# Attention kernel on one core: the values matmuls of quadrants 1 and 3 joined, and one VectorE addition put later

## Chip, core and metric

The kernel runs on one core of a Trainium2 chip. The metric is the device time of one execution in microseconds (us); lower is better. The kernel before takes 1030.06 us (median of three runs, 1028.61 to 1030.34).

## What is computed

The input is 64 sequences of 128 tokens with 512 features. The layer normalises the tokens, projects them to 16 query heads of 64 and to one shared key and value of 64, adds a null key and value, a bias per head, a causal mask and a padding mask, takes the softmax, weighs the values, projects back to 512, normalises again and adds the input:

```
xn = layernorm(x, g_in)
q = (xn @ Wq).reshape(b, n, H, DH).transpose(0, 2, 1, 3) * scale
kv = xn @ Wkv                        # k, v, with the null row ahead of each
sim = jnp.einsum('bhid,bjd->bhij', q, k) + bias      # causal and padding masks
attn = jax.nn.softmax(sim, axis=-1)
out = jnp.einsum('bhij,bjd->bhid', attn, v)
out = out.transpose(0, 2, 1, 3).reshape(b, n, INNER) @ Wo
return x + layernorm(out, g_out)
```

## The kernel before

All is float32. The 64 sequences are worked in pairs: step d (0 to 31) takes sequences a = 2d and b = 2d + 1 through scores and softmax, and the pair before, p = 2d - 2 and p + 1, through values and output projection. Each engine works its instructions in the order in which the code records them; nothing is reordered by a planner. A step is a call of `turn(d)` and then of `body_full(d)` (d = 4 to 29; earlier steps use `body`, the last two `turn_end` and `body_end`).

`turn` gives TensorE a thick run of small matmuls: `scores` (L765 to L786) for both sequences on quarters of the array, 64 rows by 64 columns, then `values` (L891 to L919) on eighths, 32 rows by 64 columns. In `values`, quadrant s of four holds 32 query tokens' weights; `turns` says in which order its blocks of keys are taken, each entry being (block j, first place, number of places). An entry with two places is one matmul of 256 columns for each half r, an entry with one place is one of 128. For s = 1 and 3, block j = 1 is two matmuls of 128; `wide` names the quadrants for which the two are made one of 256. `WIDE` (L889) names quadrant 3 alone, and `turn` (L1109, L1110) hands it to p in steps 5 to 29, and to p + 1 in the odd ones of these and in 14 and 24. So a sequence has 32 values matmuls (four rounds, four quadrants, two halves), less two for each quadrant joined.

`body_full` gives TensorE some 25 us of large matmuls: key and value projection (`kv_pair`), the query projection of the next group in a seven-product scheme (`product_two`), whose products 2, 3 and 4 are worked in the same way once more (`inner_products`), and the output projection (`out_product`), also of seven products. VectorE reads the products out of PSUM and adds them up: `inner_out` (L725) into the query tile `qT`, `q_out_two` (L621), and `out_part` (L1032) into the output `y`. Every float32 matmul that the code writes stands in the program as two weight loads and two matmuls, and both engines of the trace, PEld for loads and PE for matmuls, are fed by TensorE's one instruction stream. Some of its waits are instructions of their own: 11 in an even full step, 5 in an odd one. An even step has 780 loads and matmuls in all (772 in 14 and 24, 788 in step 4), an odd one 772.

At the end of the step, `inner_products(4, g, h, (4, 3))` (L1647) writes again into areas A0 and A1 of the fourth product's PSUM tile, which VectorE must have read by then (`inner_out(4, ...)`, L1643 and L1644). Ahead of these two readings VectorE has `q_out_two(g, h, 0, 1, "c", "u2")` (L1639), which reads another PSUM tile, `pc`.

Of the kernel before, what the change touches and what calls it, by code (L numbers as in the profile page):

```python
# [17 lines left out]
def kernel(  # L18
# [460 lines left out]
    def q_next(g, h):  # L479
        q_tiles(g, h, [q_tags[g - 1, j, h] for j in range(2)])  # L480
# [6 lines left out]
    def q_whole(g, j, u, h):  # L487
        return qT[g, j, h][:, :, :, :, u, :]
# [130 lines left out]
    def q_out_two(g, j, u, h, tag, name):  # L619
        v, k = KEPT[name]  # L620
        nc.vector.tensor_tensor(  # L621
            q_whole(g, j, u, h).rearrange("p f t h i -> p (f t h) i"),
            prod[tag].rearrange("p f (n i) -> p (f n) i", i=DH),
            q_whole(g, j, v // HC, k).rearrange("p f t h i -> p (f t h) i"),
            ALU.add,
        )
# [163 lines left out]
    def scores_add(b, hf):  # L790
        sv = S[b][:, :, KEYS[hf]].rearrange("p (r f) j -> p r f j", r=2)
        pv = pss.pop((b, hf))
        if isinstance(pv, list):
            for r in (1, 0):
                nc.vector.tensor_tensor(sv[:, r], pv[r], sv[:, r], ALU.add)  # L795
        else:
            nc.vector.tensor_tensor(sv, pv, sv, ALU.add)
# [88 lines left out]
            ps_y.tile(shape, FP, tag="X", name=f"po_{p + 1}_3"),  # L886
        ]

    WIDE = (3,)  # L889

    def values(b, wide=()):  # L891

        g, t = divmod(b, GB)
        sb = sbs.pop(b)
        po = pos[b]
        turns = (
            ((0, 0, 2), (1, 1, 1), (2, 1, 1), (3, 1, 1)),
            ((0, 0, 2), (1, 0, 1), (1, 1, 1), (2, 1, 1)),
        )
        for turn in range(len(turns[0])):  # L900
            for s in range(NQ):
                j, to, n = turns[s % 2][turn]
                if s in wide and j == 1:
                    if turn == 2:
                        continue
                    n = 2
                quad = slice(s * Q, (s + 1) * Q)
                slots = slice(2 * to + j, 2 * to + j + 2 * n - 1, 2)
                for r in range(2):
                    rows = slice(r * DH, (r + 1) * DH)  # L910
                    nc.tensor.matmul(  # L911
                        po[s][rows, to : to + n],
                        vr[g][quad, t, PLACE[j], :],
                        sb[quad, slots, r * NF : (r + 1) * NF, :],
                        start=(turn == 0),
                        stop=True,
                        skip_group_check=(turn > 0),
                        tile_position=(s * Q, r * DH),
                    )  # L919
# [144 lines left out]
    def pair_gain(b):  # L1064
        nc.vector.tensor_tensor(yn[b], yn[b], gob, ALU.mult)
# [23 lines left out]
    PAIRS = B // 2  # L1089
    late_T = []  # L1090

    def turn(d):

        a, b, p = 2 * d, 2 * d + 1, 2 * d - 2
        g = d // 2 + 1
        homes = (ps_y, "Y"), (ps_q, "a")
        if d == 1:
            homes = homes[::-1]
        scores(a, 0, (homes[0], (ps_w, "w")))
        scores(b, 0, (homes[1], (ps_w, "w")))  # L1100
        scores(a, 1)
        scores(b, 1, ((ps_y, "X"), (ps_q, "c")))
        scores_add(a, 0)
        scores_add(b, 0)
        scores_max(a, 0)
        scores_add(a, 1)
        scores_add(b, 1)
        po = values_rooms(p)
        values(p, WIDE if 4 < d < PAIRS - 1 else ())  # L1109
        values(p + 1, WIDE if 4 < d < PAIRS - 1 and (d % 2 or d % 10 == 4) else ())  # L1110
        if d % 2 and (d + 1) // 2 < NG:
            mask_neg((d + 1) // 2)
        bias_add(a + 2)
        if d % 2 == 0:
            token_sum(g, 1)
            token_sum(g, 2)
        exps(a, 0)
        values_out(p, po)
# [403 lines left out]
    def body_full(d):  # L1522

        a, b, p, l = 2 * d, 2 * d + 1, 2 * d - 2, 2 * d - 4
        g, h = d // 2 + 1, d % 2
        xw = g + 1 < NG
        m = (g + 1) * GB + 2 * h
        sums = h == 0
        q_next(g, h)
        pkv = kv_pair(g * GB + 2 * h)  # L1530
        scores_max(b, 0)
        rinv(a, 0)
        scale(a, 0)
        on = two_stats((ys[l], ys[l + 1]), "o")
        if sums:
            token_sums_inner(g, 2)
            token_sum(g, 3)
        kv_pair_out(g * GB + 2 * h, pkv)
        if h == 1 and xw:
            load_mask(g + 1)  # L1540
        nmrs[l], nmrs[l + 1] = two_nmr(*on, "o")
        if xw:
            xn = two_stats((xs[m], xs[m + 1]), "x")
        scores_max(a, 1)
        product_two(g, h, 1, ps_q, "a")
        keep_two("a", g, h, "p1")
        pair_norm(l)
        inner_room(2, g, h)
        inner_products(2, g, h, (1,))
        inner_out(2, g, h, "00")  # L1550
        exps(b, 0, 0, 1)
        scores_max(b, 1)
        if xw:
            xnmr[m], xnmr[m + 1] = two_nmr(*xn, "x")
        pair_gain(l)
        pair_residual(l)
        store(l)
        out_sum(p, 0)
        if sums:
            token_sum(g, 4)  # L1560
        out_product(p, 1, ps_y, "X")
        out_keep(p, "X", "yp1")
        out_sum(p, 1)
        out_sum(p, 2)
        exps(b, 0, 1, 4)
        product_two(g, h, 6, ps_q, "a", start=False)
        pair_norm(l + 1, (ps_y, "Y"))
        keep_two("a", g, h, "u2")
        if xw:
            norm_apply(m)  # L1570
        product_two(g, h, 5, ps_q, "c")
        exps(b, 0, 4)
        pair_gain(l + 1)
        inner_products(2, g, h, (6,))
        inner_out(2, g, h, "01")
        out_product(p, 2, ps_w, "w")
        out_part(p, 0, "w")
        out_sum(p, 3)
        if xw:
            norm_apply(m + 1)  # L1580
            tokens_T(m)
        pair_residual(l + 1)
        store(l + 1)
        rinv(b, 0)
        if xw:
            tokens_T(m + 1)
            if h == 1:
                tokens_out(g + 1)
                tokens_in(g + 1)
        for r in (p, p + 1):  # L1590
            load_res(r)
        if m + 2 < B and xw:
            load_x(m + 2)
            load_x(m + 3)
        exps(a, 1, 0, 4)
        product_two(g, h, 7, ps_q, "a", start=False)
        keep_two("a", g, h, "u3")
        inner_products(2, g, h, (7, 5, 2))
        inner_out(2, g, h, "11")
        inner_out(2, g, h, "00,11")  # L1600
        if sums:
            token_sums_inner(g, 3)
            token_sums_inner(g, 4)
        inner_room(3, g, h)
        inner_products(3, g, h, (1,))
        q_out_two(g, h, 1, 1, "c", "u3")
        inner_out(3, g, h, "00")
        out_product(p, 5, ps_y, "Y")
        exps(a, 1, 4)
        rinv(a, 1)  # L1610
        scale(a, 1)
        scale(b, 0)
        out_keep(p, "Y", "yp5")
        inner_products(3, g, h, (6, 5))
        inner_out(3, g, h, "01")
        inner_products(2, g, h, (4, 3))
        inner_out(2, g, h, "01,10")
        inner_room(4, g, h)
        inner_products(4, g, h, (1,))
        inner_out(4, g, h, "00")  # L1620
        exps(b, 1, 0, 3)
        if h == 1:
            values_T(g)
        out_product(p, 6, ps_y, "X", start=False)
        out_keep(p, "X", "yu2")
        inner_products(3, g, h, (7,))
        exps(b, 1, 3)
        blocks_T(a)
        rinv(b, 1)
        scale(b, 1)  # L1630
        bias_add(b + 2)
        if d == PAIRS - 3:
            bias_add(B - 1)
        inner_products(4, g, h, (6,))
        inner_out(4, g, h, "01")
        inner_out(3, g, h, "1*")
        inner_out(3, g, h, "*1")
        inner_products(3, g, h, (2, 3, 4))
        q_out_two(g, h, 0, 1, "c", "u2")  # L1639
        out_product(p, 7, ps_y, "X", start=False)  # L1640
        out_part(p + 1, 1, "X")
        inner_products(4, g, h, (7, 5, 2))
        inner_out(4, g, h, "11")  # L1643
        inner_out(4, g, h, "00,11")  # L1644
        out_product(p, 3, ps_y, "Y", start=False)
        out_part(p, 1, "Y")
        inner_products(4, g, h, (4, 3))  # L1647
        inner_out(4, g, h, "01,10")
        if d == PAIRS - 3:
            pair_stats(p)  # L1650
            pair_pow(p)
        blocks_T(b)
        out_product(p, 4, ps_y, "X", start=False)
        out_part(p + 1, 0, "X", False)
# [179 lines left out]
```

## Time and profile before

| | us |
|---|---|
| median of three runs | 1030.06 |
| the profiled execution | 1030.99 |
| its span from first to last instruction | 1029.2 |
| PE busy | 1019.0 |
| PEld busy | 899.0 |
| DVE busy | 860.5 |
| POOL busy | 775.3 |
| ACT busy | 674.4 |

PE is TensorE's matmuls, PEld its weight loads, DVE VectorE, ACT ScalarE, POOL GpSimd. An instruction's name gives its line in the kernel and, with an arrow, the tile that it writes and those that it reads. Idle time of an engine stands with what ended it; "issue" means that the profile shows nothing that the engine waited for. The windows view gives the length of a stretch, then each engine's busy time with the number of its instructions in brackets. Steps are cut here at the first weight load of their scores.

### The profile page before, as it was taken

How to read it: one execution, taken by the hardware profiler on the slowest of the kernel's cores; microseconds unless marked ns; L12 is line 12 of the kernel's file. 1: busy time of each engine (PE TensorE's matmuls, PEld its weight loads, DVE VectorE, ACT ScalarE, POOL GpSimd, SP SyncE). 2: the span in 40 equal slices, each digit the busy share in tenths (PEclk: the TensorE clock that was granted, in tenths of full speed). 3: DMA queues.
4: the chain of work that ended last, by engine and by line, in shares of the span. 5: the costliest groups of instructions: out<-in, count | busy, mean ns of one | idle time of the engine just before them, and what ended most of it. 6: DMA issues, size and time to landing. Idle time of an engine off the chain costs nothing.

```text
span 1029.2 us, 31577 instructions
## 1 busy us (share of the span) xinstructions
PE 1019.0 (99%) x12489; PEld 899.0 (87%) x12489; DVE 860.5 (84%) x1849; ACT 674.4 (66%) x2675; POOL 775.3 (75%) x621
## 2 busy tenths in 40 slices
PE   9999999999999999999999999999999999999997
PEld 8888888888888888888888888888988888888886
DVE  6877778888888888889888898888888888878788
ACT  5766677656577566686656776566765657856583
POOL 4997779687686876959768596786968769687686
PEclk9999999999999999999999999999999999999999
DMA  7415143151521415225152341514314152141221
GB/s 218 137 30 152 64 132 99 45 144 64 147 93 68 122 57 151 86 69 130 49 160 76 100 122 37 160 66 135 99 54 134 63 151 89 69 101 35 69 83 62
DMA packets 73835, 100.87 MB, mean 98 GB/s; under 512 B 32212, under 2 KB 36056, under 8 KB 71896
## 3 DMA queue, kind: packets, MB, share of 16 engines
q1 hardware_dynamic: 73392, 98.47, 32.1%
q8 instruction: 98, 1.61, 0.7%
q14 instruction: 49, 0.40, 0.1%
q10 hardware_dynamic: 296, 0.40, 0.1%
HBM read 63.19 MB, written 33.55 MB: 94 GB/s over the span
## 4 chain that ended last, share of the span: by engine, by line
PE 96%; POOL 1%; ACT 1%; DVE 1%; issue 1%; DMA 0%; POOLq 0%; DVEq 0%
PE pyX L998 19%; PE pa L603 13%; PE pi L697 11%; PE pyY L998 10%; PE po L911 8%; PE pkv L404 6%; PE pyw L998 5%; PE pc L603 4%; PE ps L780 3%; PE pq L499 3%; PE pa L554 2%; PE sc_X L780 2%; PE sc_Y L780 2%; PE pc L697 2%; PE pc L554 1%; PE sc_a L780 1%
## 5 line engine op out<-in xcount | busy, mean ns | idle before, releaser
L811 ACT ACTIVATE s<-s,nmax 128x65 f32<-128x65 f32 (+1 forms) x1024 | 370.9, 366 | 62.1 <-DVE nmax L802 62.1
L833 POOL TENSOR_TENSOR s<-s,rinv 128x512 f32<-128x512 f32 (+1 forms) x132 | 189.7, 1448 | 117.8 <-DVE rinv L829 117.8
L745 POOL TENSOR_TENSOR s<-biasp,mneg 128x1552 f32<-128x1552 f32 (+1 forms) x65 | 206.3, 3176 | 34.0 <-DVE s L795 22.5
L811 ACT ACTIVATION_READ_ACCUMULATOR s<-s,nmax 128x1 f32 x1024 | 194.5, 190 | 0.0
L725 DVE TENSOR_TENSOR qT<-pi,qT 128x128 f32<-128x128 f32 (+1 forms) x376 | 123.4, 340 | 39.4 <-PE pi L697 31.1
L1034 ACT COPY y<-pyX 128x256 f32<-128x256 f32 x29 | 10.8, 373 | 184.3 <-PE pyX L998 184.3
L802 DVE TENSOR_REDUCE nmax<-s 128x8 f32<-128x1032 f32 (+1 forms) x128 | 121.7, 951 | 0.1
L849 DVE STREAM_TRANSPOSE sb<-s 128x1536 f32<-128x1536 f32 (+1 forms) x68 | 113.7, 1675 | 2.1 <-POOL s L833 1.7
L998 PE MATMUL pyX<-wo,oT 128*128 128x256 f32 x464 | 109.7, 379 | 0.0
L998 PE MATMUL pyX<-wT,oT 128*128 128x256 f32 x464 | 109.7, 379 | 0.0
L978 POOL TENSOR_TENSOR oT<-oT 128x512 f32<-128x512 f32 x64 | 81.3, 1278 | 27.8 <-PE pyw L998 25.5
L998 PEld LDWEIGHTS pyX<-wo,oT 128*128 128x128 f32 x464 | 84.0, 190 | 9.2
L998 PEld LDWEIGHTS pyX<-wT,oT 128*128 128x128 f32 x464 | 84.0, 190 | 9.2
L911 PE MATMUL po<-sb,vr 32*64 32x128 f32 (+1 forms) x3904 | 88.8, 309 | 2.7 <-issue 2.4
L911 PEld LDWEIGHTS po<-sb,vr 32*64 32x64 f32 x3904 | 73.9, 131 | 15.5 <-issue 11.0
L930 ACT ACTIVATE oT<-po,nv 128x512 f32<-128x512 f32 (+1 forms) x127 | 74.1, 661 | 3.4 <-PE po L911 3.2
L404 PE MATMUL pkv<-xT,wkv 128*128 128x256 f32 x256 | 63.3, 391 | 0.0
L998 PE MATMUL pyY<-wo,oT 128*128 128x256 f32 x256 | 60.5, 379 | 0.0
L998 PE MATMUL pyY<-wT,yS 128*128 128x256 f32 x256 | 60.5, 379 | 0.0
L998 PE MATMUL pyw<-wo,oT 128*128 128x256 f32 x256 | 60.5, 379 | 0.0
L614 ACT COPY qT<-pa 128x512 f32<-128x512 f32 x78 | 45.4, 583 | 18.5 <-PE pa L603 18.3
L404 PEld LDWEIGHTS pkv<-xT,wkv 128*128 128x128 f32 x256 | 46.2, 189 | 10.0 <-DVE s L795 2.1
(231 smaller groups left out, 2509.0 us busy)
## 6 DMA issues: line engine op xcount, KB each, us to landing
res<-in_x_dram SPq DMA_DIRECT2D x64, 256.0 KB
out_dram<-y SPq DMA_DIRECT2D x63, 256.0 KB
x<-in_x_dram SPq DMA_DIRECT2D x62, 256.0 KB
xd<-xb SPq DMA_DIRECT2D x14, 1024.0 KB
xT<-xd SPq DMA_DIRECT2D x56, 256.0 KB
vr<-vd SPq DMA_DIRECT2D x64, 128.0 KB
kT<-kT SPq DMA_DIRECT2D x32, 64.0 KB
vd<-vb SPq DMA_DIRECT2D x32, 64.0 KB
```

Of the source, the lines that this page charges most:

```text
L404: nc.tensor.matmul(pkv, wkv[:, kc, :], xT[g][:, t : t + 2, kc, :], start=(kc == 0), stop=(kc == KC - 1),)
L603: nc.tensor.matmul(prod[tag][:, i], w[:, kc, f * P : (f + 1) * P], t[:, :, kc, :], start=first, stop=(kc == HK - 1), skip_group_check=not ...
L697: nc.tensor.matmul(to, inner_w[k][i][:, h], inner_x[k, g][i], start=(i == 1), stop=True, skip_group_check=(i != 1),)
L725: nc.vector.tensor_tensor(o, p, o, ALU.add)
L745: nc.gpsimd.tensor_tensor(S[b][:, :, keys], biasp[:, :, keys], mneg[:, t, keys] .unsqueeze(1) .broadcast_to([P, R8, keys.stop - keys.start ...
L780: nc.tensor.matmul(home[r][u * DH : (u + 1) * DH, f, :], qT[g, f // 2, t // 2][rows, f % 2, t % 2, hf, u], kT[rows, 0 : nk // Q, t, :], st ...
L802: nc.vector.tensor_reduce(nmax[b][:, hf], S[b][:, :, WITH_NULL[hf]], AX.X, ALU.max, negate=True)
L811: nc.scalar.activation(row, row, AF.Exp, bias=nmax[b][:, hf, k : k + 1], accum_out=rsum[b][:, hf, k : k + 1],)
L833: nc.gpsimd.tensor_tensor(sv, sv, rinvs[b, hf][:, lo:hi].unsqueeze(2).broadcast_to([P, hi - lo, sv.shape[2]]), ALU.mult,)
L849: nc.vector.transpose(sbs[b][:, :, lo:hi].rearrange("p j e q -> p e j q"), S[b][:, lo:hi, 1 : ROW - 1].rearrange("p e (j k) -> p e j k", k=Q),
L911: nc.tensor.matmul(po[s][rows, to : to + n], vr[g][quad, t, PLACE[j], :], sb[quad, slots, r * NF : (r + 1) * NF, :], start=(turn == 0), st ...
L998: nc.tensor.matmul(prod[key], h[:, c, :], w[:, c, :], start=(start and c == 0), stop=(c == HC - 1), skip_group_check=not start,)
```

## The change

```diff
-    WIDE = (3,)
+    WIDE = (1, 3)
...
-        values(p, WIDE if 4 < d < PAIRS - 1 else ())
-        values(p + 1, WIDE if 4 < d < PAIRS - 1 and (d % 2 or d % 10 == 4) else ())
+        steady = 3 < d < PAIRS - 2
+        values(p, WIDE if steady else ())
+        values(p + 1, (WIDE if d % 2 else WIDE[1:]) if steady else ())
...
-        q_out_two(g, h, 0, 1, "c", "u2")
         out_product(p, 7, ps_y, "X", start=False)
         out_part(p + 1, 1, "X")
         inner_products(4, g, h, (7, 5, 2))
         inner_out(4, g, h, "11")
         inner_out(4, g, h, "00,11")
+        q_out_two(g, h, 0, 1, "c", "u2")
         out_product(p, 3, ps_y, "Y", start=False)
```

In steps 4 to 29, p now has quadrants 1 and 3 joined, p + 1 both in an odd step and quadrant 3 in an even one. An odd step goes from 772 to 756 loads and matmuls, an even one to 764. With the waits that stand by themselves, whose number does not change, that is 761 and 775 instructions, 1536 for two steps, 768 for one on average; before it was 777 and 791 (783 in 14 and 24), 1568 for two.

TensorE, in the values of an odd step, sequence p, from the second round of `turns` on (po_0 to po_3 are the four quadrants' PSUM tiles; each row stands for the halves r = 0 and 1). Before:

```order
L911 MATMUL po_0_7945<-sb_7825,vr_7411 64x128 x2
L911 MATMUL po_1_7946<-sb_7825,vr_7411 64x128 x2
L911 MATMUL po_2_7947<-sb_7825,vr_7411 64x128 x2
L911 MATMUL po_3_7948<-sb_7825,vr_7411 64x2x128 x2
L911 MATMUL po_0_7945<-sb_7825,vr_7411 64x128 x2
L911 MATMUL po_1_7946<-sb_7825,vr_7411 64x128 x2
L911 MATMUL po_2_7947<-sb_7825,vr_7411 64x128 x2
L911 MATMUL po_0_7945<-sb_7825,vr_7411 64x128 x2
L911 MATMUL po_1_7946<-sb_7825,vr_7411 64x128 x2
L911 MATMUL po_2_7947<-sb_7825,vr_7411 64x128 x2
L911 MATMUL po_3_7948<-sb_7825,vr_7411 64x128 x2
```

TensorE at the same place, with the change:

```order
L911 MATMUL po_0_7885<-sb_7765,vr_7355 64x128 x2
L911 MATMUL po_1_7886<-sb_7765,vr_7355 64x2x128 x2
L911 MATMUL po_2_7887<-sb_7765,vr_7355 64x128 x2
L911 MATMUL po_3_7888<-sb_7765,vr_7355 64x2x128 x2
L911 MATMUL po_0_7885<-sb_7765,vr_7355 64x128 x2
L911 MATMUL po_2_7887<-sb_7765,vr_7355 64x128 x2
L911 MATMUL po_0_7885<-sb_7765,vr_7355 64x128 x2
L911 MATMUL po_1_7886<-sb_7765,vr_7355 64x128 x2
L911 MATMUL po_2_7887<-sb_7765,vr_7355 64x128 x2
L911 MATMUL po_3_7888<-sb_7765,vr_7355 64x128 x2
```

Quadrant 1's second matmul has 256 columns and its third row is gone; the columns that each quadrant streams are the same.

VectorE at the end of an even step (L725 is `inner_out`, L621 `q_out_two`, L1032 `out_part`, L849 the next transposition; pi_10_1_8192 is the fourth product's tile). Before:

```order
L725 TENSOR_TENSOR qT_1_1_8028<-pi_10_1_8167,qT_1_1_8028 128x2x2x64
L621 TENSOR_TENSOR qT_1_1_8028<-pc_1_5_8112,qT_1_1_8028 128x8x64
L1032 TENSOR_TENSOR y_8184<-pyX_1_8092,y_8184 128x256
L725 TENSOR_TENSOR qT_1_0_8027<-pi_10_1_8192,qT_1_0_8027 128x2x64
L725 TENSOR_TENSOR qT_1_0_8027<-pi_10_1_8192,qT_1_0_8027 128x2x2x64
L1032 TENSOR_TENSOR y_8097<-pyY_5_8171,y_8097 128x256
L725 TENSOR_TENSOR qT_1_0_8027<-pi_10_1_8192,qT_1_0_8027 128x4x64
L849 STREAM_TRANSPOSE sb_8252<-s_7830 128x8x6x32
```

VectorE at the same place, with the change:

```order
L725 TENSOR_TENSOR qT_1_1_7964<-pi_10_1_8103,qT_1_1_7964 128x2x2x64
L1032 TENSOR_TENSOR y_8120<-pyX_1_8028,y_8120 128x256
L725 TENSOR_TENSOR qT_1_0_7963<-pi_10_1_8128,qT_1_0_7963 128x2x64
L725 TENSOR_TENSOR qT_1_0_7963<-pi_10_1_8128,qT_1_0_7963 128x2x2x64
L621 TENSOR_TENSOR qT_1_1_7964<-pc_1_5_8048,qT_1_1_7964 128x8x64
L1032 TENSOR_TENSOR y_8033<-pyY_5_8107,y_8033 128x256
L725 TENSOR_TENSOR qT_1_0_7963<-pi_10_1_8128,qT_1_0_7963 128x4x64
L849 STREAM_TRANSPOSE sb_8188<-s_7770 128x8x6x32
```

The addition that reads `pc` stands three places later, behind the two readings of the fourth product's tile. No other engine's order changes, and no DMA moves.

## The prediction

> **What bounds the kernel now.** I read the page first: the engines' busy time, the clock, the chain that ended last and the queues.
>
> ```profile
> PE 1019.0 (99%) x12489; PEld 899.0 (87%) x12489; DVE 860.5 (84%) x1849; ACT 674.4 (66%) x2675; POOL 775.3 (75%) x621
> PEclk9999999999999999999999999999999999999999
> PE 96%; POOL 1%; ACT 1%; DVE 1%; issue 1%; DMA 0%; POOLq 0%; DVEq 0%
> q8 instruction: 98, 1.61, 0.7%
> ```
>
> TensorE is busy for 99% of the span at full clock and is 96% of the chain. So only its own work, or its own idle time, can change the time by much. The last row matters here: queue q8 brought 98 packets of instructions, 1.61 MB, so 16.4 KB each. TensorE's program has 2 x 12489 loads and matmuls and 261 others, 25239 in all; over 98 packets that is 257 to a packet. I take it as one block of 256 instructions at a time.
>
> Next the waits, all lines on the places that the change touches:
>
> ```profile
> PEld po L911 <- issue: 11.0, 44, 0.8
> PEld pi L697 <- DVE qT L725: 3.9, 13, 0.3
> PE po L911 <- issue: 2.4, 7, 0.5
> ```
>
> At the values (po, L911) TensorE stood idle 13.4 us and waited for nothing that the profile shows, up to 0.8 us at a time. At the fourth product (pi, L697) it waited for VectorE. To see how much of the first is loss, I cut the span at steps with the windows view (length, then busy time and count by engine):
>
> ```profile
> 185.85:970.45 784.60, 782.10 (x9691) 691.20 (x9690) 667.00 (x1449) 519.53 (x2047) 584.21 (x467) 1.00 0.32 96
> 154.83:185.85 31.02, 31.02 (x396) 27.56 (x395) 26.75 (x58) 20.28 (x81) 28.34 (x26) 1.00 0.28 87
> 342.64:374.62 31.98, 31.46 (x392) 27.75 (x391) 26.54 (x59) 20.41 (x81) 28.51 (x27) 1.00 0.28 89
> 595.25:626.46 31.21, 31.21 (x392) 27.71 (x391) 27.11 (x59) 20.38 (x81) 28.52 (x27) 1.00 0.28 90
> 626.46:658.05 31.59, 31.50 (x387) 27.66 (x386) 26.96 (x60) 21.43 (x83) 18.70 (x12) 1.00 0.38 105
> 658.05:689.10 31.05, 31.05 (x392) 27.59 (x391) 27.18 (x59) 20.29 (x81) 28.51 (x26) 1.00 0.29 93
> 689.10:720.18 31.08, 31.08 (x387) 27.54 (x386) 26.86 (x60) 21.31 (x83) 18.71 (x12) 1.00 0.39 111
> 782.31:814.14 31.83, 31.44 (x387) 27.74 (x387) 26.71 (x59) 20.29 (x81) 28.56 (x26) 1.00 0.27 86
> ```
>
> The first row is steps 5 to 29 together; then come steps 4, 10, 18, 19, 20, 21 and 24. Undisturbed, an even step takes 31.05 us (step 20) and an odd one 31.08 (step 21), yet equal work takes up to 31.98 (step 10). The 25 steps in the first row would take 13 x 31.08 + 12 x 31.05 = 776.6 us undisturbed; they took 784.60. So **8.0 us** is lost in them. The timeline of weight loads shows where:
>
> ```profile
> 285.41 0.22 PEld L911 LDWEIGHTS po<-sb,vr 32*64 32x64 f32 x11 [0.67 <-issue]
> 348.28 0.44 PEld L911 LDWEIGHTS po<-sb,vr 32*64 32x64 f32 x27 [0.77 <-issue]
> 788.05 0.19 PEld L911 LDWEIGHTS po<-sb,vr 32*64 32x64 f32 x3 [0.63 <-issue]
> 850.34 0.41 PEld L911 LDWEIGHTS po<-sb,vr 32*64 32x64 f32 x19 [0.22 <-issue]
> ```
>
> In the middle of the values, between two loads of one kind, the stream stops for 0.2 to 0.8 us, each time at another place (11, 27, 3, 19 loads are left). I counted what lies from gap to gap:
>
> ```profile
> 285.40:348.27 62.87, 62.35 (x760) 55.11 (x760) 53.55 (x119) 41.61 (x164) 47.20 (x39) 1.00 0.33 99
> 788.04:850.33 62.29, 62.28 (x760) 55.07 (x760) 52.95 (x117) 40.97 (x162) 46.67 (x38) 1.00 0.33 100
> ```
>
> Both times 760 loads: with as many matmuls and the 16 waits that two steps hold, 1536 instructions, six blocks of 256. The gaps stand at the seams of the blocks that q8 brings: the stream has run dry. Before the change two steps hold 1568, so a seam falls 32 earlier in each later pair of steps, and drifts through the thick run of scores and values.
>
> **The seams after the change.** Two steps hold 1536, so every even step has its seams where step 4 has them, which nothing ahead of it moves. Loads from the start of steps 4, 18, 19, 20 and 21 to a gap:
>
> ```profile
> 154.82:285.40 130.58, 129.94 (x1798) 115.20 (x1797) 113.17 (x244) 86.51 (x346) 99.38 (x79) 1.00 0.34 99
> 595.24:788.04 192.80, 192.33 (x2574) 170.50 (x2573) 167.61 (x362) 128.28 (x510) 146.75 (x118) 1.00 0.33 100
> 626.45:788.04 161.59, 161.12 (x2184) 142.80 (x2183) 140.50 (x304) 107.90 (x429) 118.23 (x91) 1.00 0.34 102
> 658.04:788.04 130.00, 129.63 (x1798) 115.13 (x1797) 113.54 (x245) 86.47 (x346) 99.53 (x80) 1.00 0.34 101
> 689.09:788.04 98.95, 98.58 (x1408) 87.55 (x1407) 86.36 (x187) 66.19 (x265) 71.02 (x53) 1.00 0.35 103
> ```
>
> Step 4: 2 x 1797 and 34 waits are 3628 = 14 x 256 + 44, so its seams stand at instructions 44, 300 and 556, early in the scores, early in the values and in the body. Step 20 has the same count, so the same seams; both took the undisturbed time (31.02 and 31.05). The odd steps follow 775 instructions later, 7 over three blocks, so their seams stand at 37, 293 and 549. By the same count (23, 39 and 50 waits) step 21 has 21 and 277 and lost nothing; step 19 has 53 and 309 and lost 31.59 - 31.08 = 0.51 us; step 18, an even one, has 76 and 332 and lost 0.16. An odd step's 37 lies midway between 21 and 53: I take 0.2 us left for each of 13 odd steps and none for the even ones, 2.6 us. The bounds are 0 (all like steps 20 and 21) and 0.51 x 13 + 0.16 x 13 = 8.7 us.
>
> The Trainium skill, page "Runtime: NRT & Kernel Launch", section "Instruction fetch mechanics", gives the same block, 16 KiB or 256 instructions. It also says that crossing such a boundary is "mostly hidden"; the gaps of 0.63 to 0.77 us at the seams speak against that here. What it would give is the first rival.
>
> **The joined matmuls.** 102 matmuls of the code are saved, 408 instructions, 25239 to 24831. The columns stay. Does the values block itself get shorter? Undisturbed blocks with none, two and four joined, each row pair from its first load to that of the next kind:
>
> ```profile
> 157.67 2.28 PEld L911 LDWEIGHTS po<-sb,vr 32*64 32x64 f32 x128 [0.17 <-issue]
> 160.12 0.94 PEld L404 LDWEIGHTS pkv<-xT,wkv 128*128 128x128 f32 x5 [0.17 <-DVE s L795]
> 660.89 2.31 PEld L911 LDWEIGHTS po<-sb,vr 32*64 32x64 f32 x124 [0.17 <-issue]
> 663.37 0.94 PEld L404 LDWEIGHTS pkv<-xT,wkv 128*128 128x128 f32 x5 [0.17 <-DVE s L795]
> 691.94 2.29 PEld L911 LDWEIGHTS po<-sb,vr 32*64 32x64 f32 x120 [0.17 <-issue]
> 694.40 0.94 PEld L404 LDWEIGHTS pkv<-xT,wkv 128*128 128x128 f32 x5 [0.17 <-DVE s L795]
> ```
>
> 128 loads take 2.45 us, 124 take 2.48, 120 take 2.46: the columns set the time, not the number of instructions. I count the joining by itself at **0**. It is covered by the other quadrants' streaming; the ends are 26 x 0.03 = +0.8 us (as from 128 to 124) and, if instructions set it after all, 204 loads x 2.31/124 = -3.8 us. The rows name 0.17 us ahead of the values in each step; that stays, and is no part of the 8.0.
>
> **The areas read sooner.** The end of an even (748) and an odd step (779), TensorE and then VectorE:
>
> ```profile
> 747.13 1.89 PE L998 MATMUL pyY<-wo,oT 128*128 128x256 f32 x8
> 749.40 0.38 PE L998 MATMUL pyX<-wT,oT 128*128 128x256 f32 x1
> 778.15 1.89 PE L998 MATMUL pyY<-wo,oT 128*128 128x256 f32 x8
> 780.49 0.38 PE L998 MATMUL pyX<-wT,oT 128*128 128x256 f32 x1
> ```
>
> ```profile
> 748.00 0.74 DVE L725 TENSOR_TENSOR qT<-pi,qT 128x128 f32<-128x128 f32 x2
> 778.21 0.69 DVE L621 TENSOR_TENSOR qT<-pc,qT 128x512 f32<-128x512 f32 x1
> 779.14 0.74 DVE L725 TENSOR_TENSOR qT<-pi,qT 128x128 f32<-128x128 f32 x2
> 780.08 0.42 DVE L1032 TENSOR_TENSOR y<-pyY,y 128x256 f32<-128x256 f32 x1 [0.19 <-PE pyY L998]
> ```
>
> Eight matmuls at 0.216 us (the eight from 747.13 end by 749.02, 0.38 of it the last one's own length: 1.51 / 7) and four half as wide at 0.111 us (an estimate: half of the first and 3 ns) are 2.17 us; from the first pyY to pyX it was 2.27 and 2.34. TensorE loses 0.10 us in an even step and 0.17 in an odd one, since the four matmuls between were due at 748.86 and 779.88, their first weight load ahead of that, and the two L725 for which it waits end only at 748.74 and 779.88. With L621 (0.69 us) behind them they end some 0.6 us sooner, 748.1 and 779.3, and the wait goes: 13 x 0.10 + 13 x 0.17 = **3.5 us** over steps 4 to 29. What is late next? L621 would end at about 779.9, and L1032 behind it starts at 780.08, when TensorE has ended pyY, so it is not moved. Nothing needs `pc` or that part of `qT` before the next scores, over 2 us on.
>
> **The sum**, against the profiled execution: 1030.99 - 8.0 + 2.6 + 0 - 3.5 = 1022.1 us. The last two steps get other seams too; a gap there can come or go, at most the 0.77 us of the timeline each, and I count them at nothing. The median shown is 0.9 below that execution, so I predict **1021.2 us**, and 1018.6 to 1024.6 for this case (0 to 6 us left at the seams).
>
> **Rivals.** (1) The gaps are not the fetching of blocks, as the page's rule would have it, and remain: only the 3.5 us go, 1030.1 - 3.5 = 1026.5. Against it stand the two counts of 760 loads from gap to gap, and step 4's count, which reaches the gap at 285.41 with the same remainder, 44, as step 20's that at 788.05. 10%. (2) The seams come to rest where the stream always runs dry: the place is the values of all 26 steps, the price that of step 24, 31.83 - 31.05 = 0.78 us. Then it is 1030.1 - 8.0 - 3.5 + 26 x 0.78 = 1038.9, and it turns slower from (8.0 + 3.5) / 26 = 0.44 us a step. Step 19 paid more than that with its seam 16 further on; steps 4, 20 and 21 speak against it. 5%. (3) The wait for VectorE stays, because L1032 ahead of the two L725 is as late: 1021.2 + 3.5 = 1024.7. Against it: the pyX that L1032 reads stands ahead of the pyY of 747.13 and 778.15 in TensorE's order. 7%. (4) The block shortens by the 3.8 us as well: 1017.4. 5%. My forecast has the other 73%.
>
> **Range and chances.** A measurement can tell about 0.2%, 2.1 us, from no change. Leaving out (2) and the far ends, the range is 1017.5 to 1027.0. Faster 0.91: all but (2) and part of (1) and of the bad end of the seams; the same 0.04; slower 0.05.
>
> **What would show it.** Right: steps of 30.9 to 31.2 us that no longer wander, no row of 0.6 us of issue inside the values, the issue wait at po down from 13.4 us to 5 to 8, the L697 wait for VectorE gone, 97 packets on q8. Wrong: one and the same gap in every odd step at instruction 293, or in every even one at 300; a wait at the first scores for `y` or `qT`; blocks of values away from 2.45 to 2.5 us.

## The result, and the profile after

| kernel | us, median | lowest to highest | runs |
|---|---|---|---|
| before | 1029.63 | 1028.61 to 1030.34 | 6 |
| with the change | 1022.94 | 1022.45 to 1023.09 | 6 |

The ratio is 0.9936, with a 95% interval of 0.9923 to 0.9948: 6.7 us faster, where 1021.2 us was predicted. The profiled execution took 1022.45 us, its span 1020.6, against 1030.99 and 1029.2 before: 8.5 us less.

The page of the changed kernel, in the same lines (engines, chain, instruction queue):

```profile
PE 1012.9 (99%) x12285; PEld 902.0 (88%) x12285; DVE 860.8 (84%) x1849; ACT 672.8 (66%) x2675; POOL 775.0 (76%) x621
PE 95%; ACT 2%; POOL 1%; DVE 1%; issue 0%; DMA 0%; POOLq 0%; DVEq 0%
q8 instruction: 96, 1.57, 0.6%
```

204 loads and 204 matmuls are gone and q8 brought two packets less. TensorE is the bound as before. Its weight loads were busy for 902.0 us, 3.0 more than before, although there are fewer of them: 2.2 of that stand at the inner products (pi: 132.8 us before, 135.0 now, and 134.9 in experiment 1 below, where only the addition moves), 0.9 at the values (po: 73.9 and 74.8). Loads that overlap are counted once in a busy time, so it does not tell what the change cost; the length of the steps does.

The waits on TensorE at the places that the change touches are down to one row:

```profile
PEld po L911 <- issue: 5.3, 31, 0.2
```

It was 11.0 us in 44 waits of up to 0.8 us. Now it is 0.17 us once in each step that has values, the entry into them that the change was not expected to move. The wait of the fourth product for VectorE (pi L697) has no row any more.

Steps 4, 5, 20 and 21, and then steps 4 to 29 together, in the windows view of the changed kernel (length, busy time and count by engine):

```profile
154.74:185.76 31.02, 31.02 (x383) 27.74 (x383) 26.69 (x58) 20.32 (x81) 28.28 (x26) 1.00 0.28 89
185.76:216.84 31.08, 31.08 (x379) 27.79 (x379) 26.80 (x60) 21.31 (x83) 18.61 (x13) 1.00 0.39 108
651.54:682.56 31.02, 31.02 (x383) 27.75 (x382) 27.16 (x59) 20.30 (x81) 28.65 (x27) 1.00 0.31 100
682.56:713.64 31.08, 31.08 (x379) 27.79 (x378) 26.81 (x60) 21.31 (x83) 18.59 (x13) 1.00 0.39 109
154.74:962.04 807.30, 807.30 (x9881) 721.89 (x9880) 694.00 (x1506) 538.25 (x2128) 612.10 (x492) 1.00 0.33 97
```

The steps no longer wander: 13 x 31.02 + 13 x 31.08 = 807.30, which is the whole stretch to the hundredth. TensorE is busy in all of it. No step has a gap at a seam. But 31.02 and 31.08 are also what undisturbed steps took before (31.05 for an even step with one sequence joined). The wait for VectorE is gone from them, 0.10 and 0.17 us, and yet they are no shorter. So something else costs as much.

That something is in the values. Blocks of steps 4 and 5, from the first load to that of the next kind:

```profile
157.58 2.39 PEld L911 LDWEIGHTS po<-sb,vr 32*64 32x64 f32 x116 [0.17 <-issue]
160.13 0.94 PEld L404 LDWEIGHTS pkv<-xT,wkv 128*128 128x128 f32 x5 [0.17 <-issue]
188.60 2.46 PEld L911 LDWEIGHTS po<-sb,vr 32*64 32x64 f32 x112 [0.17 <-issue]
191.23 0.94 PEld L404 LDWEIGHTS pkv<-xT,wkv 128*128 128x128 f32 x5 [0.17 <-issue]
```

116 loads take 160.13 - 157.58 = 2.55 us and 112 take 2.63. Before, 120 to 128 loads took 2.45 to 2.48. With fewer matmuls for the same columns the block is **longer**. (From unrounded starts the first is 2.56, the value used below.)

The wait that went: TensorE and then VectorE at the end of step 5.

```profile
212.84 1.89 PE L998 MATMUL pyY<-wo,oT 128*128 128x256 f32 x8
214.57 0.38 PE L697 MATMUL pi<-xI,wq 128*128 128x128 f32 x2
214.79 0.39 PE L697 MATMUL pi<-xS,wR 128*128 128x128 f32 x2
215.02 1.89 PE L998 MATMUL pyX<-wT,oT 128*128 128x256 f32 x8
```

```profile
213.05 0.75 DVE L725 TENSOR_TENSOR qT<-pi,qT 128x128 f32<-128x128 f32 x2
213.71 0.68 DVE L621 TENSOR_TENSOR qT<-pc,qT 128x512 f32<-128x512 f32 x1
214.77 0.42 DVE L1032 TENSOR_TENSOR y<-pyY,y 128x256 f32<-128x256 f32 x1 [0.39 <-PE pyY L998]
```

VectorE has read the areas by 213.80, 0.77 us before TensorE writes there at 214.57, and from the first pyY to pyX it is 2.18 us instead of 2.34. L621 ends at 214.39, and L1032 behind it still waits 0.39 us for pyY: the moved addition delays nothing.

### The profile page after: what moved, and what is told of

Same layout as the page of the kernel before. It is cut to its first block, busy times and chain, and to the rows that moved or that the text cites. A ratio compares the mean times of both kernels' runs of the same rounds, so it can differ in the third digit from the quotient of the medians.

```text
span 1020.6 us, 31143 instructions
## 1 busy us (share of the span) xinstructions
PE 1012.9 (99%) x12285; PEld 902.0 (88%) x12285; DVE 860.8 (84%) x1849; ACT 672.8 (66%) x2675; POOL 775.0 (76%) x621
## 3 DMA queue, kind: packets, MB, share of 16 engines
q8 instruction: 96, 1.57, 0.6%
## 4 chain that ended last, share of the span: by engine, by line
PE 95%; ACT 2%; POOL 1%; DVE 1%; issue 0%; DMA 0%; POOLq 0%; DVEq 0%
PE pyX L998 20%; PE pa L603 13%; PE pi L697 11%; PE pyY L998 10%; PE po L911 8%; PE pkv L404 6%; PE pyw L998 5%; PE pc L603 4%; PE ps L780 3%; PE pq L499 3%; PE pa L554 2%; PE sc_X L780 2%; PE sc_Y L780 2%; PE pc L697 2%; ACT s L811 2%; PE pc L554 1%
## 5 line engine op out<-in xcount | busy, mean ns | idle before, releaser
L725 DVE TENSOR_TENSOR qT<-pi,qT 128x128 f32<-128x128 f32 (+1 forms) x376 | 123.6, 340 | 35.9 <-PE pi L697 28.8
L849 DVE STREAM_TRANSPOSE sb<-s 128x1536 f32<-128x1536 f32 (+1 forms) x68 | 113.6, 1674 | 2.1 <-POOL s L833 1.7
L911 PE MATMUL po<-sb,vr 32*64 32x128 f32 (+1 forms) x3700 | 86.2, 315 | 0.1
L911 PEld LDWEIGHTS po<-sb,vr 32*64 32x64 f32 x3700 | 74.8, 131 | 9.5 <-issue 5.3
L930 ACT ACTIVATE oT<-po,nv 128x512 f32<-128x512 f32 (+1 forms) x127 | 73.9, 660 | 0.4 <-PE po L911 0.4
```

The source lines that it names most:

```text
L725: nc.vector.tensor_tensor(o, p, o, ALU.add)
L849: nc.vector.transpose(sbs[b][:, :, lo:hi].rearrange("p j e q -> p e j q"), S[b][:, lo:hi, 1 : ROW - 1].rearrange("p e (j k) -> p e j k", k=Q),
L911: nc.tensor.matmul(po[s][rows, to : to + n], vr[g][quad, t, PLACE[j], :], sb[quad, slots, r * NF : (r + 1) * NF, :], start=(turn == 0), st ...
```

## The experiments

The theory to test: blocks of 256 instructions arrive late where a seam falls into the thick run, the change puts the seams at 44 and 300 (even steps) and 37 and 293 (odd), where it costs nothing; the moved addition gives 3.5 us; the joining takes about as much back. The first rival for the seams is that gaps go because there are fewer instructions; for the blocks, several.

**1. The addition alone.** The kernel before, with only the moved line:

```diff
-        q_out_two(g, h, 0, 1, "c", "u2")
         out_product(p, 7, ps_y, "X", start=False)
...
         inner_out(4, g, h, "00,11")
+        q_out_two(g, h, 0, 1, "c", "u2")
```

> The kernel before with the VectorE addition moved and the joins as they were. Terms apart: the wait at the fourth product goes in all 26 steps, 13 x 0.10 + 13 x 0.17 = 3.5 us, and the seams keep drifting, so the gaps in the values stay near the 8.0 us of before: 1029.6 - 3.5 = 1026.1, 1025 to 1027.5. Rival (the move also takes the gaps away, because VectorE is ready sooner for the next step): 1026.1 - 8.0 = 1018.1. Rival (the move is worth nothing): 1029.6.

Measured: 1027.26 us (12 runs), before on the same chip 1030.33; ratio 0.9970, interval 0.9961 to 0.9979. Steps 4, 5 and 10, and steps 4 to 29:

```profile
154.84:185.76 30.92, 30.92 (x396) 27.65 (x395) 26.75 (x58) 20.28 (x81) 28.25 (x26) 1.00 0.28 87
185.76:216.67 30.91, 30.91 (x387) 27.63 (x386) 26.78 (x60) 21.30 (x83) 18.59 (x13) 1.00 0.40 109
341.91:374.50 32.59, 31.61 (x391) 27.96 (x390) 26.16 (x59) 20.41 (x81) 28.61 (x27) 1.00 0.28 88
154.84:967.85 813.01, 809.04 (x10085) 720.60 (x10085) 691.09 (x1506) 539.36 (x2128) 611.74 (x492) 1.00 0.32 96
```

An undisturbed step is 0.10 (even) and 0.17 us (odd) shorter than before, as predicted. The gaps still wander, up to 32.59 us for a step; undisturbed, the 26 steps would make 804.1 us (30.92 for step 4, 30.94 for the other even steps, which have one sequence joined, as step 28 took, and 30.91 for the odd ones, from unrounded times), so the gaps are 813.01 - 804.1 = 8.9 us. So neither the move nor the wait that it removes has to do with the gaps.

**2. The joining alone.** The changed kernel, with that line back in its old place.

```diff
+        q_out_two(g, h, 0, 1, "c", "u2")
         out_product(p, 7, ps_y, "X", start=False)
...
         inner_out(4, g, h, "00,11")
-        q_out_two(g, h, 0, 1, "c", "u2")
```

> The changed kernel with the VectorE addition back in its old place. Terms apart: the steps stay at 1536 instructions for two, no gap comes back, and the wait at the fourth product does, 3.5 us: 1022.9 + 3.5 = 1026.4, 1025.8 to 1027, steps of 31.12 (even) and 31.25 us (odd), each the same. Rival (seams hold only because the moved addition lets the stream run ahead at a step's end): gaps of up to 0.5 us in the odd steps come back, 1026.4 + 6 = 1032.

Measured: 1026.35 us (1026.15 to 1026.72), ratio 0.9962, interval 0.9950 to 0.9974. Steps 4 and 5, and 4 to 29:

```profile
154.87:186.00 31.13, 31.13 (x383) 27.66 (x382) 26.69 (x58) 20.32 (x81) 28.29 (x26) 1.00 0.27 88
186.00:217.26 31.26, 31.26 (x379) 27.70 (x378) 26.90 (x60) 21.30 (x83) 18.72 (x12) 1.00 0.39 109
154.87:965.82 810.95, 810.95 (x9881) 719.78 (x9880) 695.07 (x1506) 538.06 (x2128) 611.76 (x493) 1.00 0.33 96
```

No gap is left (the counts, not the move, fix the seams), and the steps are 0.11 and 0.18 us longer than with both parts. The two parts add up: 0.9970 x 0.9962 = 0.9932, with 0.9936 for both.

**3. The seams elsewhere.** The joining begins three steps earlier. Each steady step has the same instructions as with the change; only the seams stand at 132 and 388 and at 125 and 381, in the middle of the scores and of the values.

```diff
-        steady = 3 < d < PAIRS - 2
+        steady = 0 < d < PAIRS - 2
```

> The changed kernel with steps 1 to 3 joined as well: 88 fewer instructions ahead of step 4, so the seams of all steps 4 to 29 move from 44 and 300 (even) and 37 and 293 (odd) to 132 and 388, and 125 and 381; everything else in these steps is the same. Seam theory: each of the 26 steps pays what steps of before with such seams paid, 0.3 to 0.6 us (steps 13 to 15, seams at 141, 132 and 117, lost 0.57, 0.35 and 0.32): 8 to 16 us more, 1031 to 1039, with the gap always at the same load of the values. Rival (the gaps went because the joined values have fewer instructions, wherever the seams are): the joins of three more steps cost 0.4 us, 1023.3.

Measured: 1029.17 us (1027.85 to 1030.98), ratio 0.9993, interval 0.9982 to 1.0004. Step 6's loads:

```profile
220.21 1.37 PEld L911 LDWEIGHTS po<-sb,vr 32*64 32x64 f32 x65 [0.17 <-issue]
222.15 1.07 PEld L911 LDWEIGHTS po<-sb,vr 32*64 32x64 f32 x51 [0.57 <-issue]
223.38 0.73 PEld L404 LDWEIGHTS pkv<-xT,wkv 128*128 128x128 f32 x4 [0.17 <-DVE rinv L829]
```

The values of an even step begin at instruction 258; 65 loads and 65 matmuls on is 388, and there the stream stops for 0.57 us. Joining more matmuls, the kernel gave back the whole gain: steps 4 to 29 took 813.44 us, 6.1 more than with the change. So it is the place and not the number of instructions. The size is 0.24 us a step on the mean, less than I expected. Where the stream stops, it is at the same load in all even steps (65) and in all odd ones (62), but it does not always stop: steps 5, 23, 25 and 27 took the undisturbed 31.08 us. The place makes a stop possible; experiment 12 shows what else it takes.

**4. A seam a little on.** One step earlier only, which puts the seams at 76 and 332 and at 69 and 325.

```diff
-        steady = 3 < d < PAIRS - 2
+        steady = 2 < d < PAIRS - 2
```

> The changed kernel with step 3 joined as well: 32 fewer instructions ahead of step 4, so the seams of steps 4 to 29 stand at 76 and 332 (even) and 69 and 325 (odd). Seam theory: gaps come back, small in the even steps (step 18 of before, seams at 76 and 332, lost 0.16) and larger in the odd ones (steps 17 and 19, at 85 and 53, lost 0.63 and 0.51); with the seams at 132 the steps lost 0.2 on average where before had led me to 0.3 to 0.6, so I halve: 13 x 0.08 + 13 x 0.28 = 4.7 us, and 0.2 for the joins of step 3: 1027.8, 1024 to 1031. Rival (the gaps need the second seam to be late in the values, and 332 is early): no gap, 1023.1.

Measured: 1025.2 us (1024.75 to 1025.34), ratio 0.9958, interval 0.9941 to 0.9974. Gaps come back, in 9 of the 26 steps and up to 0.37 us, 1.8 us in all. The direction is as expected, the size less than half.

**5. Both joined in one round?** The changed kernel with quadrant 3's joined matmul a round later where both are joined.

```diff
-                if s in wide and j == 1:
+                if s == 3 and len(wide) == 2 and turn:
+                    if turn == 3:
+                        continue
+                    j, to, n = ((2, 1, 1), (1, 0, 2))[turn - 1]
+                elif s in wide and j == 1:
```

> The changed kernel with quadrant 3's joined matmul one round later where quadrants 1 and 3 are both joined: round 2 has quadrant 1 joined and 3 single, round 3 has quadrant 3 joined and none of 1, and no round has only quadrants 0 and 2. Same instructions, seams and columns. If the values grew (by 0.08 us in an even step and 0.17 in an odd one) because both joined quadrants are busy at once while a round holds only 0 and 2, most of these 3.2 us go: 1019.7 to 1021.5. Rival (each joined matmul of quadrant 1 costs its time wherever it stands): 1022.9, and blocks of 2.56 and 2.63 us as before the stagger.

Measured: 1023.5 us (1023.41 to 1023.63), ratio 0.9934, interval 0.9922 to 0.9946; blocks 2.56 and 2.63 us as before. Two joined matmuls in one round are not what costs.

**6. Quadrant 1 alone.** The first experiment with the other quadrant joined.

```diff
-    WIDE = (3,)
+    WIDE = (1,)
```

> The kernel before with the VectorE addition moved, and quadrant 1 joined in place of quadrant 3 (same steps, same number of joins, same seams as before). It tells what makes a block of values longer. If a joined matmul of quadrant 1 costs by itself: an undisturbed block with one joined sequence takes 2.45 + 0.08 = 2.53 us and with two 2.62. If the time grows only where both quadrants are joined: 2.48 and 2.47, as with quadrant 3 alone. The whole time tells nothing here, since the gaps drift: 1025 to 1029.

One execution: 1030.13 us, with wandering gaps as before. Its undisturbed blocks in steps 4, 5 and 6, with none, two and one of the two sequences joined:

```profile
157.75 2.28 PEld L911 LDWEIGHTS po<-sb,vr 32*64 32x64 f32 x128 [0.17 <-issue]
160.20 0.94 PEld L404 LDWEIGHTS pkv<-xT,wkv 128*128 128x128 f32 x5 [0.17 <-DVE s L795]
188.66 2.53 PEld L911 LDWEIGHTS po<-sb,vr 32*64 32x64 f32 x120 [0.17 <-issue]
191.36 0.73 PEld L404 LDWEIGHTS pkv<-xT,wkv 128*128 128x128 f32 x4 [0.17 <-issue]
219.81 2.43 PEld L911 LDWEIGHTS po<-sb,vr 32*64 32x64 f32 x124 [0.17 <-issue]
222.41 0.73 PEld L404 LDWEIGHTS pkv<-xT,wkv 128*128 128x128 f32 x4 [0.17 <-issue]
```

2.45, 2.70 and 2.60 us. With quadrant 3 in its place, the rows in the prediction gave 2.45, 2.46 and 2.48. So quadrant 1's join costs 0.13 to 0.15 us a sequence by itself and quadrant 3's next to nothing. What sets the two apart in the code is their place in the order, 3 being the last in a round, and their rows of the array, 32 to 63 and 96 to 127; experiment 11 tells the two apart.

**7. The joined ones first.** In the rounds after the first, where both are joined:

```diff
-            for s in range(NQ):
+            for s in (1, 3, 0, 2) if len(wide) == 2 and turn else range(NQ):
```

> The changed kernel with the quadrants taken in the order 1, 3, 0, 2 in the rounds after the first, where both are joined. Same instructions, columns and seams. The last weight loads of a block of the changed kernel are quadrant 3's, the quadrant that streams its joined matmul latest. If the block grew since the last matmuls of quadrant 3 are left over alone at the end, joined quadrants first should bring blocks back towards 2.47 us: 1019.7 to 1022. Rival (the columns of a quadrant and its joined matmul set the time, in any order): blocks of 2.56 and 2.63 us, 1022.9.

Measured: 1025.06 us (1024.9 to 1025.81), ratio 0.9960, interval 0.9947 to 0.9972. Blocks of steps 4 and 5:

```profile
157.68 2.47 PEld L911 LDWEIGHTS po<-sb,vr 32*64 32x64 f32 x116 [0.17 <-issue]
160.32 0.73 PEld L404 LDWEIGHTS pkv<-xT,wkv 128*128 128x128 f32 x4 [0.17 <-issue]
188.78 2.56 PEld L911 LDWEIGHTS po<-sb,vr 32*64 32x64 f32 x112 [0.17 <-issue]
191.52 0.51 PEld L404 LDWEIGHTS pkv<-xT,wkv 128*128 128x128 f32 x3 [0.17 <-issue]
```

2.64 and 2.74 us: longer still. The order matters.

**8. The last round turned round.** If what costs were matmuls left over at the end, the order of the last round would change it.

```diff
-            for s in range(NQ):
+            for s in (3, 2, 1, 0) if wide and turn == 3 else range(NQ):
```

> The changed kernel with the quadrants of the last round of each joined sequence taken in the order 3, 2, 1, 0. Same instructions, columns and seams. If the left-over matmuls of quadrant 3 make the block's end, this takes 0.1 us off it in each step, 1020.3; if the block's end is set by something other than the order, 1022.9.

Measured: 1023.85 us (1023.64 to 1024.1), ratio 0.9947, interval 0.9934 to 0.9959; blocks 2.64 and 2.63 us. No gain, so that theory falls.

**9. The joined ones last.** The opposite of experiment 7:

```diff
-            for s in range(NQ):
+            for s in (0, 2, 1, 3) if len(wide) == 2 and turn else range(NQ):
```

> In a sequence with both quadrants joined, each round after the first goes through the quadrants in the order 0, 2, 1, 3, so that the two joined matmuls come last in their round instead of second and fourth; the seams stay at 44 and 300, 37 and 293. Theory, order: a joined matmul holds back what is issued behind it in its round (joined last in the order, quadrant 3 alone cost nothing; quadrant 1 alone 0.12 us; both put first, blocks of 2.64 and 2.73 us). Then the blocks go from 2.56 and 2.63 back to 2.48 to 2.50 us, the steps lose 13 x 0.07 + 13 x 0.14 = 2.7 us, and the time is 1022.9 - 2.7 = 1020.2. Rival, columns: quadrant 1's 256 columns cost wherever they stand, since its rows have no other work to be spread over: blocks of 2.56 and 2.63 as now and 1022.9.

Measured: **1018.9 us** (1018.58 to 1019.34, 4 runs), before on the same chip 1029.1; ratio 0.9905, interval 0.9890 to 0.9920, below the interval of the change. Its blocks and steps (4 and 5, and 4 to 29):

```profile
157.64 2.27 PEld L911 LDWEIGHTS po<-sb,vr 32*64 32x64 f32 x116 [0.17 <-issue]
160.08 0.94 PEld L404 LDWEIGHTS pkv<-xT,wkv 128*128 128x128 f32 x5 [0.17 <-DVE s L795]
188.55 2.27 PEld L911 LDWEIGHTS po<-sb,vr 32*64 32x64 f32 x112 [0.17 <-issue]
190.99 1.16 PEld L404 LDWEIGHTS pkv<-xT,wkv 128*128 128x128 f32 x6 [0.17 <-DVE s L795]
```

```profile
154.80:185.71 30.91, 30.91 (x384) 27.64 (x383) 26.75 (x58) 20.28 (x81) 28.26 (x26) 1.00 0.28 88
185.71:216.59 30.88, 30.88 (x379) 27.60 (x378) 26.76 (x60) 21.31 (x83) 18.59 (x13) 1.00 0.40 107
154.80:958.08 803.28, 803.28 (x9881) 718.13 (x9880) 693.90 (x1506) 538.02 (x2128) 612.12 (x492) 1.00 0.33 97
```

The blocks are 2.44 us in both kinds of step, a little under those with nothing joined, and the steps take 803.28 us instead of 807.30. With the joined matmuls behind the narrow ones of their round, joining costs nothing, and both gains are kept. This version beats the kernel before and the changed one.

**10. The same order everywhere**, also in the first round and in sequences with one or no quadrant joined. It takes one wait out of TensorE's stream early on, so that all seams stand one instruction later, at 45 and 301, 38 and 294.

```diff
-            for s in range(NQ):
+            for s in (0, 2, 1, 3):
```

> The order 0, 2, 1, 3 in all rounds and all sequences, joined or not; the seams move by one instruction, to 45 and 301, 38 and 294. Theory, order: as with the joined last in the later rounds, blocks of 2.48 to 2.50 us and 1020.2 us; if what counts is that each quadrant waits the same number of places from round to round (in the run before this one quadrant 1 moves back a place between its first and second round), it is better still, 2.45 us and 1019.0. Rival, columns: 2.56 and 2.63 us, and 1022.9.

Measured: 1023.03 us (1022.64 to 1025.57), ratio 0.9948, interval 0.9936 to 0.9961. The odd steps have blocks of 2.45 us, as the order would have it; the even ones of 2.51 to 3.06, changing from step to step. Neither theory had foreseen that.

**11. The two joined ones exchanged.**

```diff
-            for s in range(NQ):
+            for s in (0, 2, 3, 1) if len(wide) == 2 and turn else range(NQ):
```

> As in the run with the joined last (blocks of 2.44 us in every step, 1018.9 us), but the two joined matmuls change places: order 0, 2, 3, 1 in the rounds after the first where both are joined. Seams unchanged. Theory, joined behind the narrow ones of their round: which of the two comes first does not matter, blocks of 2.44 to 2.46 us and 1018.9. Rival, quadrant 1's join is free only where quadrant 3's follows it: blocks of 2.5 us or more and 1020.5 or more.

Measured: 1019.74 us (1019.64 to 1020.03), ratio 0.9912, interval 0.9898 to 0.9925; blocks of 2.46 to 2.47 us, and one small gap in one step. Nearly all of the gain is there: it is enough that both stand behind the narrow ones. Quadrant 1, in the same rows of the array, costs next to nothing here, so it was its place in the order. Quadrant 3 last is 0.03 us a block better, which the theory did not give.

**12. One instruction.** Experiment 9's steady steps, with the order 0, 2, 1, 3 also in the steps that join nothing (0 to 3, 30 and 31), so that the seams stand one instruction later and nothing else differs in steps 4 to 29.

```diff
-            for s in range(NQ):
+            for s in (0, 2, 1, 3) if not wide or len(wide) == 2 and turn else range(NQ):
```

> The steady steps as in the run with the joined last, but the steps ahead of them, which join nothing, go through the quadrants in the order 0, 2, 1, 3; that drops one wait early on, so that every seam stands one instruction later: 45 and 301, 38 and 294. In the run with order 0, 2, 1, 3 everywhere the even steps lost 0.1 to 0.6 us each (3.1 us in all) and the odd ones nothing. Theory, place: it is the seam at 301 instead of 300, and the even steps lose 3 us here too, steps of 31.0 to 31.5, time 1018.9 + 3 = 1022. Rival, order: the even steps lost it to the order in their first round and in their second sequence, and one instruction makes no difference: no gap, 1018.9.

Measured: 1023.95 us (1022.09 to 1025.63), ratio 0.9954, interval 0.9939 to 0.9968. Steps 4, 5 and 6, and 4 to 29; then step 6's loads:

```profile
154.82:186.07 31.25, 31.25 (x383) 27.80 (x382) 26.70 (x58) 20.52 (x81) 28.27 (x26) 1.00 0.28 88
186.07:216.96 30.89, 30.89 (x379) 27.60 (x378) 26.78 (x60) 21.30 (x83) 18.61 (x13) 1.00 0.39 105
216.96:248.44 31.48, 31.33 (x383) 27.80 (x382) 26.92 (x59) 20.41 (x81) 28.61 (x27) 1.00 0.30 94
154.82:962.05 807.23, 807.03 (x9881) 719.77 (x9880) 693.20 (x1506) 539.63 (x2128) 611.62 (x492) 1.00 0.33 97
```

```profile
219.80 0.64 PEld L911 LDWEIGHTS po<-sb,vr 32*64 32x64 f32 x22 [0.17 <-issue]
220.82 1.83 PEld L911 LDWEIGHTS po<-sb,vr 32*64 32x64 f32 x94 [0.38 <-issue]
222.82 1.16 PEld L404 LDWEIGHTS pkv<-xT,wkv 128*128 128x128 f32 x6 [0.17 <-DVE rinv L829]
```

The odd steps are those of experiment 9; the even ones lose 4.0 us. The stream stops after 22 loads: 258 instructions, 22 loads and 21 matmuls are 301, the seam. So experiment 10's loss was the place too and not the order.

The transfers of q8 show what happens. Here are the q8 rows of the DMA view, which gives for a stretch each queue's packets, megabytes and time: first of the 0.9 us from step 6's first load on in experiment 9 (216.59 to 217.49), then of 217.86 to 218.50 in this run. Its step 6 starts at 216.96, and it has no q8 row in the 0.9 us from there:

```profile
q8 instruction: 1, 0.02, 8.6%
q8 instruction: 1, 0.02, 13.7%
```

The block comes later. In the 13 even steps of experiment 9, the last packet before the values starts between 0.07 us ahead of the step's first load and 0.83 us behind it, and has ended by 1.78 us; here it starts at 0.90 to 1.44 us and ends at 1.78 to 2.54. Experiment 10 is like this run: 0.89 to 1.65. In step 6 the loads go on 1.32 us after the packet's end.

The changed kernel's even steps stand one instruction short of that place; whether its own order of quadrants would lose there as well was not tried.

## Why the prediction was right or wrong

**The sum.** For the profiled execution it gave 1022.1 us; it took 1022.45. But two of its terms were wrong and offset each other.

- *8.0 us of gaps go*: right. Undisturbed steps of 31.02 (step 4), 31.05 and 31.08 us make 807.6 in steps 4 to 29, and before took 815.62 there. That the gaps stand at seams of 256 instructions is borne out by experiments 3 and 12, in which the seams alone were put elsewhere and the stops came at the instruction counted (388, 301).
- *2.6 us left in the odd steps*: wrong in size, 0. I had put 0.2 us on the seam at 293 because it lies between 277, which cost nothing, and 309, which cost 0.51. All 13 odd steps took 31.08 us without a stop. Experiment 12 shows why reading off between two places does not work: 300 costs nothing and 301 up to 0.6. Nor does one step give the price of a place. Steps 25, 27 and 29 of before had seams at 477, 445 and 413, deep in the values, and took 31.08 us like step 21; and the seam at 309, from which I took 0.51 us, cost 0.70 in experiment 1 and nothing in experiment 6.
- *Joining at 0*: this step failed. Its reason, "covered by the other quadrants' streaming", came from rows with quadrant 3 alone. Against the undisturbed steps of experiment 1, 804.1 us, the change took 807.30: **+3.2 us**, far beyond the upper end of +0.8. Experiments 6, 7 and 9 show that it hangs on the place of the joined matmul in its round, not on the joining: 2.44 us with it last, 2.56 and 2.63 in the order of the code, 2.64 and 2.74 with it first. The direction of the lower end, a shorter block by fewer instructions, was wrong altogether.
- *3.5 us of wait go*: right. The wait is gone in every step, and experiment 1 has steps that are 0.10 and 0.17 us shorter.
- *The last two steps at 0*: right; from step 30 to the end of the span it was 58.6 us, and 58.75 before.

So -8.0 - 3.5 + 3.2 = -8.3 us in steps 4 to 29, as the windows have it (815.62 to 807.30). That the sum came out so near is luck: 2.6 us too much for the seams stood against 3.2 too little for the joining.

**From the profiled execution to the median.** I took 0.9 us off, as before's profiled execution was that much over its median. The changed kernel's was 0.5 under. With the 0.35 of the sum that is the miss: 0.35 + 0.9 + 0.5 = 1.7. Before's executions took 1026.68 to 1031.71 in 23 runs on one chip, while the changed kernel's lie within 0.64 us. That the spread is the gaps that each happened to have is likely, not shown. An offset taken from a kernel with wandering gaps does not carry over to one without.

**The rivals.** (1), gaps that are not the fetching of blocks, falls by experiments 3 and 12 and by the times of the q8 packets (last section). The Trainium skill's rule for it (page "Runtime: NRT & Kernel Launch", section "Instruction fetch mechanics", a crossing is "mostly hidden") holds in this kernel only at some places: nothing is lost at 300 with the change, and a stop of 0.57 us is seen at 388 in experiment 3. (2), seams that rest at a bad place, did not come true here, but experiment 3 makes it real: it took the whole gain, at 0.24 us a step instead of the 0.78 that I had put on it. (3) falls, the wait is gone. (4) has the wrong sign.

**What would show it.** Of the marks, the constant steps, the issue wait of 5.3 us (5 to 8 predicted) and the vanished wait came; q8 had 96 packets for 97. The mark for wrong, "blocks of values away from 2.45 to 2.5 us", came as well, and it pointed at the step that failed.

## What to carry to other kernels

When equal steps take unequal time and the engine that bounds them waits for nothing that is shown, count its instructions from gap to gap; if it is a multiple of 256, the number of instructions in the steady loop decides where the seams fall, and 88 instructions far ahead moved the time by 0.6% here (experiment 3), a single one by 0.5% (experiment 12 against 9). Try several places on the chip rather than reckon between two known ones. When narrow matmuls are joined in a packed group, try the joined ones behind the narrow ones of their round, and check the group's length, not its number of instructions.

## What the runs showed that I had not expected

- One instruction is enough: the same steady steps took 803.28 us with the even steps' seams at 44 and 300 and 807.23 with them at 45 and 301. The odd steps took 30.89 us with 293 and with 294. It is not that the seam parts a load from its matmul, as it does at 301: it does so at 293 too, which cost nothing. What goes before the loss is that the block is fetched some 0.8 us later (experiment 12). Why it is, and whether the seam at 45 or that at 301 is the cause, the runs do not show.
- The same place costs nothing or half a microsecond, as the block's packet ends sooner or later. In before and experiments 1, 3, 4, 6, 10 and 12 the loads of the values stop for over 0.15 us 68 times in steps 4 to 29. Each time they go on 1.23 to 1.57 us after the end of the last q8 packet, whose transfer takes 0.9 to 2.0 us. This ties the stops to the fetching of blocks more closely than the counts. It also shows how little room the even steps have at 300: in experiment 11 the step with the small gap, 20, is the one whose packet ended last, 1.97 us after the step's first load.
- Equal columns in fewer matmuls can take longer. The values block took 2.45 us with 128 loads, 2.63 with 112 in one order and 2.44 with 112 in another. Part of it can be placed: in step 5 of the changed kernel the block's first 54 loads start within 0.04 us of those of experiment 9, and then the last two of the first sequence come at 1.12 us instead of 0.98. What holds them the trace does not say; that a joined matmul holds back those issued behind it fits experiments 6, 7, 9 and 11, but is argued, not shown. It does not say why turning the last round's narrow matmuls round made the even steps' block 0.08 us longer (experiment 8).
